# Layer 1's loop with four engine queues tied to program order, and a step that starts with work from the step before

## The chip, the cores and the metric

The program runs on one core of one Trainium2 chip. The metric is the device time of one execution in microseconds; the kernel before takes 18878.0 us (median of three runs, 18847.7 to 18889.9). A core has five instruction queues that matter here: PE (matmul and transpose), DVE (vector), ACT (scalar, activation functions), POOL (GpSimd) and SP, which issues most of the DMA transfers. Each engine runs its own stream of instructions and waits on semaphores where it needs another engine's result.

## The reference, cut to what matters

The input x has the shape (4, 512, 512, 16). Each layer normalises by groups of two channels, applies a convolution and adds its input. Layer 0 is a global convolution in the Fourier domain. The change concerns layer 1 alone, a 3x3 convolution whose output passes through an arc cosine and two tanh factors:

```python
input_norm = jnp.sqrt(lax.conv_general_dilated(x * x, ones_f, strides, 'SAME', ...) + EPS)
kernel_norm = jnp.sqrt(jnp.sum(kernel * kernel, axis=(0, 1, 2), keepdims=True) + EPS)
y = lax.conv_general_dilated(x, kernel / kernel_norm, strides, 'SAME', ...)
y = y / input_norm
y = 1.0 - jnp.arccos(y) * (2.0 / jnp.pi)
y = y * (jnp.tanh(kernel_norm / radius) * jnp.tanh(input_norm / radius))
...
x = x + _L1_conv_ref(_gn(x), ...)
```

The group norm needs mean and variance over a whole image, so the statistics of an image must be complete before its first block enters layer 1. The arc cosine is evaluated as a square root times a polynomial in |y|.

## The kernel before

The program runs the phases of layer 0 (filter, forward, convolution in frequency), then `last_phase`: an inverse transform that writes the layer-0 result by channel to DRAM (L1096 to L1108), and then the loop of layer 1, which starts at about 17116 us of the span. Only this loop is touched.

**Beside the loop: `prepare()` (L994).** A Python generator makes x + layer 0 for every image and its statistics. For one tile of 128 rows by 128 columns it loads x and two halves of the layer-0 result (`p_x`, `p_y`, L1001 and L1005, two buffers each), adds them on POOL (L1026, twice), takes 16 bn_stats on DVE (L1022), and writes the tile to DRAM (`t_d`, L1034). After 16 tiles it aggregates and finishes the image's mean and variance (L1041 to L1068). Image 0 is finished before the loop. The statistics of the other three images run beside it: one `next(beside, None)` (L1331) per step.

**The loop.** The output of an image is cut into groups of 32 columns and four units of 128 rows each: 256 units in 64 groups over four images. Input comes in blocks of eight columns by 16 channels, transposed so that the partitions hold (column, channel). Each unit passes through these functions, and a step u of `step(u)` (L1300) runs each of them for a different unit, so that 14 units are in flight (`lead = 14`):

- `block` (L1134): four transposes on PE (L1138), the normalising activation to `xn` on ACT (L1146), its square `x2` (L1148), a memset on POOL (L1144).
- `squares` (L1159): four matmuls on PE (L1164) that sum squares over channels, a copy on DVE to `e_sum` (L1168), and in two steps of four a small copy on POOL (L1170, L1173).
- `over_w` (L1175) and `norms` (L1181), once per group: two additions on POOL (L1177, L1178), three matmuls on PE (L1185 to L1187), a square root and, for every second group, tanh on ACT (L1192, L1194), a reciprocal on DVE (L1196).
- `border` (L1207), once per group: copies on POOL (L1214), four transposes on PE (L1217), memsets on POOL, and three operations on DVE (L1226).
- `conv` (L1230): 12 matmuls (24 in the profile[...]; L1234) and one for the edges (L1242), into the PSUM tile `pc`, of which there are four.
- `cosine` (L1250): one multiplication on DVE (L1252).
- `root` (L1255): Abs, Relu and Sqrt on ACT (L1258 to L1260). `factors` (L1263): three Squares and a Sign on ACT (L1268, L1270).
- `gate` (L1273) and `signed` (L1278): one multiplication each on POOL (L1275, L1280).
- `chain` (L1282): five dependent operations on DVE (three on L1286, then L1287 and L1289), which read and write the PSUM tile and end with `e_o`.
- `finish` (L1292): an addition on POOL (L1294) and the output DMA on SP (L1296).

**What sets the order.** The program is written for a framework that records instructions and dependences, and whose scheduler then orders every engine's instructions by its own estimate of when each becomes ready, with program order as priority. Python order in `step` therefore does not fix the order on an engine. In the program before, pieces of different steps are mixed: transposes stand between the matmuls of a conv, and the chains of two units alternate on DVE. Buffers are handed out in turn: `pc` has four, `e_y` and `e_sum` four, `e_v` and `e_o` three, `e_q`, `e_gate`, `pt` two, and the sums of squares `p2` one.

Of the kernel before, what the change touches and what calls it, by code (L numbers as in the profile page):

```python
# [199 lines left out]

def bc(ap, axis, shape):
    return ap.unsqueeze(axis).to_broadcast(shape)

# [711 lines left out]
def last_phase(tc, cst, x, y_d, yw_d, t_d, kern, bias, radius, out):  # L917
    nc = tc.nc
    with ExitStack() as ctx:
# [71 lines left out]
        order = [0, 2, 1, 3]  # L991
# [81 lines left out]
        beside = prepare()  # L1073
# [47 lines left out]
        n_groups = 16 * B  # L1121
        n_units = 4 * n_groups
# [3 lines left out]
        def load(g):  # L1126
            t = xp.tile([P, 4, 32, C], F32, name="xt")
            b, wt, w = order[g // 16], g % 16 // 4, g % 4 * 32
            nc.sync.dma_start(
                out=t, in_=t_d[b][wt].rearrange("(h p) w c -> p h w c", p=P)[:, :, w : w + 32, :]  # L1130
            )
            xt[g] = t

        def block(q):  # L1134

            pt = ps_t.tile([P, N], F32, name="pt")
            for h in range(4):
                nc.tensor.transpose(  # L1138
                    pt[:, h * P : (h + 1) * P],
                    xt[q // 4][:, h, q % 4 * 8 : q % 4 * 8 + 8, :].rearrange("p w c -> p (w c)"),  # L1140
                    ident,
                )
            xn = np_.tile([P, N + 2], F32, name="xn")
            nc.gpsimd.memset(xn[:, 0 : N + 2 : N + 1], 0.0)  # L1144
            vec = vecs[order[q // 64]]
            nc.scalar.activation(xn[:, 1 : N + 1], pt, AF.Identity, scale=vec[:, 0:1], bias=vec[:, 1:2])  # L1146
            x2 = ew.tile([P, N], F32, name="x2")
            nc.scalar.activation(x2, xn[:, 1 : N + 1], AF.Square)  # L1148
            xns[q], x2s[q] = xn, x2
# [9 lines left out]
        def squares(q):  # L1159

            g, k = q // 4, q % 4
            p2 = ps_s.tile([P, 4, 8], F32, name="p2", tag="gn_ps")
            for h in range(4):
                nc.tensor.matmul(p2[:, h], x2s[q][:, h * P : (h + 1) * P], cols, start=True, stop=True)  # L1164
            del x2s[q]
            if g not in sums:
                edges(g)
            nc.vector.tensor_copy(sums[g][:, :, 1 + 8 * k : 9 + 8 * k], p2)  # L1168
            if k == 0 and g % 16 > 0:
                nc.gpsimd.tensor_copy(sums[g - 1][:, :, 33:34], sums[g][:, :, 1:2])  # L1170
            if k == 3 and g % 16 < 15:
                edges(g + 1)
                nc.gpsimd.tensor_copy(sums[g + 1][:, :, 0:1], sums[g][:, :, 32:33])  # L1173
# [7 lines left out]
        def norms(g):  # L1181

            s3 = st["s3"]
            pn = ps_n.tile([P, 4, 32], F32, name="pn")
            nc.tensor.matmul(pn, over_h[:, 0], s3, start=True, stop=False)  # L1185
            nc.tensor.matmul(pn[:, 1:4], over_h[:, 1], s3[:, 0:3], start=False, stop=False)
            nc.tensor.matmul(pn[:, 0:3], over_h[:, 2], s3[:, 1:4], start=False, stop=True)  # L1187
            if g % 2 == 0:
                st["inn"] = ew.tile([P, 2, 4, 32], F32, name="l_inn")
                st["th"] = ew.tile([P, 2, 4, 32], F32, name="l_th", bufs=4)  # L1190
            inn, th = st["inn"], st["th"]
            nc.scalar.activation(inn[:, g % 2], pn, AF.Sqrt, bias=eps1)  # L1192
            if g % 2:
                nc.scalar.activation(th, inn, AF.Tanh, scale=rrad)  # L1194
            rin = ew.tile([P, 4, 32], F32, name="l_rin", bufs=4)
            nc.vector.reciprocal(rin, inn[:, g % 2])  # L1196
            rins[g], ths[g] = rin, th[:, g % 2]
# [9 lines left out]
        def border(g):  # L1207

            t = ew.tile([P, 4, 3, 2, C], F32, name="e_bx")
            for side in range(2):  # L1210
                at, w = (g + 2 * side - 1, 31 - 31 * side)
                if at // 16 != g // 16 or at < 0:
                    at, w = g, 0
                nc.gpsimd.tensor_copy(t[:, :, :, side], bc(xt[at][:, :, w, :], 2, [P, 4, 3, C]))  # L1214
            pt = ps_t.tile([P, N], F32, name="pt")
            for h in range(4):
                nc.tensor.transpose(pt[:96, h * P : (h + 1) * P],  # L1217
                                    t[:, h].rearrange("p d s c -> p (d s c)"), ident)
            bx = ew.tile([96, N], F32, name="e_bn")
            nc.gpsimd.memset(bx[0:32, 0:1], 0.0)  # L1220
            nc.gpsimd.memset(bx[64:96, N - 1 : N], 0.0)
            vec = vecs[order[g // 16]]
            for dh in range(3):
                r = slice(32 * dh, 32 * dh + 32)
                lo, hi = max(1 - dh, 0), min(N + 1 - dh, N)
                nc.vector.tensor_scalar(bx[r, lo:hi], pt[r, lo + dh - 1 : hi + dh - 1],  # L1226
                                        vec[r, 0:1], vec[r, 1:2], ALU.mult, ALU.add)
            borders[g] = bx

        def conv(u):  # L1230
            h, ts = u % 4, list(terms(u // 4))
            pc = ps_c.tile(sh, F32, name="pc")
            for n, (q, dh, lo, hi, o) in enumerate(ts):
                nc.tensor.matmul(  # L1234
                    pc[:, lo:hi, :].rearrange("p w j -> p (w j)"),
                    xns[q][:, h * P + dh : h * P + dh + P],
                    bands[dh][:, o : o + hi - lo, :].rearrange("p w j -> p (w j)"),
                    start=(n == 0), stop=False,
                )

            lo, hi = int(u // 4 % 16 == 0), 2 - int(u // 4 % 16 == 15)
            nc.tensor.matmul(  # L1242
                pc[:, 31 * lo : 31 * hi - 30 : 31, :],
                borders[u // 4][:, h * P : (h + 1) * P], eband[:, lo:hi], start=False, stop=True,
            )
            if h == 3:
                del borders[u // 4]
            pcs[u] = pc
# [6 lines left out]
        def root(u):  # L1255

            v = ew.tile(sh, F32, name="e_v", bufs=3)
            nc.scalar.activation(v, st["y", u], AF.Abs)  # L1258
            nc.scalar.activation(v, v, AF.Relu, scale=-1.0, bias=1.0)
            nc.scalar.activation(pcs[u], v, AF.Sqrt, scale=ARC[7] ** 2)  # L1260
            st["v", u] = v
# [16 lines left out]
        def signed(u):  # L1278
            t = st["gate", u]
            nc.gpsimd.tensor_mul(t, t, st.pop(("y", u)))  # L1280

        def chain(u):  # L1282

            r = pcs.pop(u)
            for q, (_, rest) in zip(st.pop(("q", u)), ARC_PAIRS):
                nc.vector.scalar_tensor_tensor(r, q, rest, r, ALU.add, ALU.mult)  # L1286
            nc.vector.scalar_tensor_tensor(r, st.pop(("v", u)), ARC_ROOT - 1.0, r, ALU.add, ALU.mult)  # L1287
            o = ew.tile(sh, F32, name="e_o", bufs=3)
            nc.vector.scalar_tensor_tensor(o, r, -1.0, st.pop(("gate", u)), ALU.add, ALU.mult)  # L1289
            st["o", u] = o  # L1290
# [7 lines left out]
        lead = 14  # L1298

        def step(u):  # L1300
            if u % 4 == 0 and (u + lead) // 4 + 2 < n_groups:
                load((u + lead) // 4 + 2)
            if 0 <= u + lead - 1 < n_units:
                squares(u + lead - 1)

            g, k = divmod(u + lead - 3 - 4, 4)
            if k == 0 and 0 <= g < n_groups:
                norms(g)
            if u + lead < n_units:
                block(u + lead)  # L1310
            if u % 4 == 2 and 0 <= u + 6 < n_units:
                border((u + 6) // 4)
            if 0 <= u + 3 < n_units:
                conv(u + 3)
            if 0 <= u < n_units:
                signed(u)
            if 0 <= u - 1 < n_units:
                finish(u - 1)
            if 0 <= u + 1 < n_units:
                root(u + 1)  # L1320
                gate(u + 1)
                factors(u + 1)
            if 0 <= u < n_units:
                chain(u)
            if 0 <= u + 2 < n_units:
                cosine(u + 2)
            g, k = divmod(u + lead - 2 - 4, 4)
            if k == 0 and 0 <= g < n_groups:
                over_w(g)
            if u >= 0:  # L1330
                next(beside, None)  # L1331
            for q in [q for q in xns if q < u]:
                del xns[q]

# [1 line left out]
            next(beside)  # L1336
        for g in range(3):
            load(g)
        for u in range(-lead, n_units + 1):
            step(u)  # L1340


def body(tc, ins, cst, out):
# [47 lines left out]
```

## Time and profile before

| | |
|---|---|
| median of three runs | 18878.0 us |
| profiled execution | 18884.85 us, its span 18883.1 us |
| PE busy over the span | 17055.0 us (90%) |
| DVE, ACT, POOL busy | 11526.1 (61%), 9724.0 (51%), 11616.7 us (62%) |
| mean granted PE clock | 0.957 |
| layer-1 loop, first transposes to the end | 17116 to 18883 us |

The span is the profiler's own window of the execution; some 2 us of the execution lie around it. Busy shares of the whole span are means over phases with different limits: in the loop of layer 1, from 17154 us on, PE, DVE and ACT are all busy most of the time. Rows of a timeline give the start and the duration in us, the engine, the line, the operation with its output and inputs, and in brackets the idle time before it and what ended that idle time. A list of waits gives the total in us, how often, and the longest.

### The profile page before, as it was taken

Reading aid. Unit: us, or ns where it says so; the run is one execution under the profiler, and the core shown is the slowest. Engines: PE = TensorE matmul, PEld = TensorE weight load, DVE = VectorE, ACT = ScalarE, POOL = GpSimd, SP = SyncE. Lnnn points to the kernel's source line nnn. Section 1 sums busy time; section 2 is a strip of 40 time slices with the busy share of each in tenths; the row PEclk is TensorE's granted clock in tenths of the full one; section 3 lists DMA queues with packets and bytes.
Section 4 is the critical chain, followed back from the end, with each engine's and each line's share of the span. In section 5 each row is a group of like instructions: output and inputs, shape, how many; then the busy total and the mean of one; then the engine's idle time right before and its main releaser. Section 6 shows DMA issues by size and latency. Waiting matters only on the chain. (4 is left out here: it accounts for less than half of the span.)

```text
span 18883.1 us, 533095 instructions
## 1 busy us (share of the span) xinstructions
PE 17055.0 (90%) x224908; PEld 12368.5 (66%) x224908; DVE 11526.1 (61%) x24155; ACT 9724.0 (51%) x17871; POOL 11616.7 (62%) x12701
## 2 busy tenths in 40 slices
PE   7899999999998998988888888888898988988898
PEld 5455555555554457777777777777777776877777
DVE  8877777777773335555555555555555555246887
ACT  4455555555552235555555555555555554005788
POOL 7577777777771126666666666666666666026776
PEclk8899999999999999999999999999999999998999
DMA  3755555455547668888888888888888888696432
GB/s 101 207 153 141 144 150 150 134 152 152 147 140 230 187 199 321 325 319 320 322 323 318 324 318 320 322 323 321 323 322 320 324 324 306 248 326 208 161 127 71
DMA packets 2918838, 4543.16 MB, mean 241 GB/s; under 512 B 117634, under 2 KB 2086492, under 8 KB 2809566
## 3 DMA queue, kind: packets, MB, share of 16 engines
q1 hardware_dynamic: 2686254, 3768.92, 59.1%
q0 software_dynamic: 174896, 605.89, 8.3%
q10 hardware_dynamic: 55296, 134.24, 2.1%
q8 instruction: 1773, 29.05, 0.6%
q14 instruction: 619, 5.07, 0.1%
HBM read 3031.24 MB, written 1477.31 MB: 239 GB/s over the span
## 5 line engine op out<-in xcount | busy, mean ns | idle before, releaser
L783 PE MATMUL pg<-c_dg,g 64*128 64x128 f32 x32832 | 2855.2, 291 | 347.3 <-ACT gh L683 193.2
L799 PE MATMUL pm<-xe,gh 128*32 128x64 f32 x131328 | 2394.6, 222 | 555.4 <-issue 297.3
L799 PEld LDWEIGHTS pm<-xe,gh 128*32 128x32 f32 x131328 | 2011.6, 111 | 1153.2 <-issue 962.1
L783 PEld LDWEIGHTS pg<-c_dg,g 64*128 64x128 f32 x32832 | 2292.4, 190 | 695.3 <-issue 257.2
L372 PE MATMUL pg<-c_dinv,sp 128*128 128x256 f32 x8192 | 2279.4, 426 | 296.0 <-ACT st L377 179.1
L828 DVE TENSOR_TENSOR z<-zq,pz 128x256 f32<-128x256 f32 x2052 | 861.8, 420 | 2665.9 <-ACT zq L827 2591.7
L348 DVE RECIPROCAL dn<-dn 128x256 f32<-128x256 f32 x1024 | 1790.8, 1749 | 774.7 <-POOL dn L341 774.6
L372 PEld LDWEIGHTS pg<-c_dinv,sp 128*128 128x128 f32 x8192 | 1611.1, 207 | 944.3 <-issue 213.0
L681 DVE COPY gh<-pg 128x512 f32<-128x512 f32 x2046 | 1410.0, 689 | 1247.7 <-PE pg L783 1244.0
L417 PE MATMUL pt<-ev_in,c_todd 128*128 128x512 f32 x4096 | 1974.9, 607 | 51.9 <-DMA ev_in<-g_d 27.3
L752 POOL TENSOR_TENSOR xu<-xe,c_late 128x256 f32<-128x256 f32 x2052 | 1393.7, 705 | 893.1 <-ACT xe L683 866.3
L683 ACT COPY yf<-pm 128x512 f32<-128x512 f32 x2046 | 1210.9, 592 | 935.8 <-PE pm L799 921.5
L335 ACT COPY ab<-pab 128x512 f32<-128x512 f32 x2048 | 1103.9, 591 | 1126.3 <-POOL m L355 323.9
L377 ACT COPY st<-pg 128x256 f32<-128x256 f32 x2048 | 1072.6, 622 | 1025.4 <-PE pg L372 629.3
L763 ACT COPY xe<-xl 64x1024 f32<-64x1024 f32 x513 | 538.6, 1050 | 1891.4 <-POOL xl L754 1891.4
L350 POOL TENSOR_TENSOR x<-ab,ab 128x256 f32<-128x256 f32 x1024 | 874.7, 854 | 922.9 <-ACT ab L335 896.4
L683 ACT COPY gh<-pg 128x512 f32<-128x512 f32 x2058 | 1201.1, 584 | 392.3 <-PE pg L783 383.0
L820 PE MATMUL pz<-c_ident,yf 128*128 128x128 f32 x8208 | 1373.7, 290 | 29.8 <-issue 28.0
L417 PEld LDWEIGHTS pt<-ev_in,c_todd 128*128 128x128 f32 x4096 | 807.5, 198 | 680.0 <-issue 518.2
L329 PEld LDWEIGHTS pab<-c_e,u 18*128 18x128 f32 x8192 | 719.0, 187 | 806.1 <-ACT st L377 458.3
L754 POOL TENSOR_TENSOR xl<-xl,xu 128x1024 f32<-128x1024 f32 x513 | 1209.7, 2358 | 40.2
L329 PE MATMUL pab<-c_e,u 18*128 18x256 f32 x8192 | 1186.5, 406 | 5.6 <-ACT ab L335 5.6
(205 smaller groups left out, 33831.8 us busy)
## 6 DMA issues: line engine op xcount, KB each, us to landing
xe<-xf_d SPq DMA_DIRECT2D x1026, 1536.0 KB, 10.7
g<-g_d SPq DMA_DIRECT2D x511, 1024.0 KB, 9.9
g_d<-st SPq DMA_DIRECT2D x64, 4096.0 KB, 34.5
ev_in<-g_d SPq DMA_DIRECT2D x1024, 256.0 KB, 4.8
g_d<-ot SPq DMA_DIRECT2D x1024, 256.0 KB, 2.8
xf_d<-xe POOLq DMA_DIRECT2D x513, 448.0 KB, 8.4
xf_d<-xl POOLq DMA_DIRECT2D x513, 448.0 KB, 5.4
x_d<-xo SPq DMA_DIRECT2D x128, 1024.0 KB, 5.1
```

Source lines behind the costliest of these rows:

```text
L329: nc.tensor.matmul(pp[n][:, k].rearrange("p c n -> p (c n)"), w["us"][n][q, k1 : k1 + P], e2[q, n, w["h"], :], start=True, stop=True,)
L335: nc.scalar.copy(w["ab"][n], pp[n])
L348: nc.vector.reciprocal(w["dn"], w["dn"])
L372: nc.tensor.matmul(pg[:, k].rearrange("p a x -> p (a x)"), w["sp"][:, k, c, :], dinv[:, 2 * kp + k, c, :], start=(c == 0), stop=(c == 1),)
L417: nc.tensor.matmul(pt, todd[:, c, kc, hh * P : hh * P + P], ev[:, kc, c], start=(kc == 0), stop=(kc == 1),)
L681: nc.vector.tensor_copy(dst, src)
L683: nc.scalar.copy(dst, src)
L752: nc.gpsimd.tensor_mul(u[:, :, h, c], xe[:, :, h, 1 - c], bc(late[:, 1 + c], 2, [P, F, 2]))
L754: nc.gpsimd.tensor_add(xl.rearrange("p f h c k -> p (f h c k)"), xl.rearrange("p f h c k -> p (f h c k)"), u.rearrange("p f h c k -> p (f ...
L783: nc.tensor.matmul(pg[c][:, j % 4], g[half, j], dg[half], start=True, stop=True)
L799: nc.tensor.matmul(pm[32 * q : 32 * q + 32, g % 8], gh[:, f].rearrange("p c j -> p (c j)"), xe[:, :, f].rearrange("p t h c k -> p t (h c k ...
L820: nc.tensor.transpose(pz[:, t % 4].rearrange("p v q x -> p (v q x)"), y[:, at].rearrange("p g x -> p (g x)"), ident)
```

## The change

A small class ties the instructions that a block of code records to program order on chosen engines. Each instruction of such an engine gets an ordering edge to the one recorded before it on the same engine; the edge adds no semaphore. The loop runs `step(u)` inside it, with PE, DVE, ACT and POOL chosen. SP is not chosen. The load of a group and `next(beside, None)` move out of `step` and stay untied. Inside `step` the written order, which now is the order on each engine, is changed: `signed(u)`, `chain(u)` and `root(u + 1)`, whose inputs come from the step before, stand first.

```diff
+class InOrder:
+    def __init__(self, tc, *engines):
+        self.tc, self.last, self.depth = tc, {}, 0
+        self.engines = [e.engine for e in engines]
+
+    def __enter__(self):
+        self.begin = len(self.tc.nc.cur_bb.bb.instructions)
+
+    def __exit__(self, *_):
+        dep = mybir.DependencyInfo(mybir.DependencyClass.NoSync, mybir.DependencyReason.DATA)
+        for i in list(self.tc.nc.cur_bb.bb.instructions)[self.begin :]:
+            if i.engine in self.engines:
+                if i.engine in self.last:
+                    self.tc.add_manual_dep(i, self.last[i.engine], dep, reason="in order")
+                self.last[i.engine] = i.name
...
         def step(u):
-            if u % 4 == 0 and (u + lead) // 4 + 2 < n_groups:
-                load((u + lead) // 4 + 2)
+            if 0 <= u < n_units:
+                signed(u)
+                chain(u)
+            if 0 <= u + 1 < n_units:
+                root(u + 1)
             if 0 <= u + lead - 1 < n_units:
                 squares(u + lead - 1)
...
                 conv(u + 3)
-            if 0 <= u < n_units:
-                signed(u)
             if 0 <= u - 1 < n_units:
                 finish(u - 1)
             if 0 <= u + 1 < n_units:
-                root(u + 1)
                 gate(u + 1)
                 factors(u + 1)
-            if 0 <= u < n_units:
-                chain(u)
             if 0 <= u + 2 < n_units:
                 cosine(u + 2)
...
                 over_w(g)
-            if u >= 0:
-                next(beside, None)
...
+        pinned = InOrder(tc, nc.tensor, nc.vector, nc.scalar, nc.gpsimd)
         for u in range(-lead, n_units + 1):
-            step(u)
+            if u % 4 == 0 and (u + lead) // 4 + 2 < n_groups:
+                load((u + lead) // 4 + 2)
+            with pinned:
+                step(u)
+            if u >= 0:
+                next(beside, None)
```

So the order on each engine within a step becomes, in the program as built: PE squares, norms, block, border, conv; DVE chain, the copy of the squares, reciprocal, border, cosine; ACT root, the norms' square root and tanh, block, factors; POOL signed, the small copies, memset, border copies, finish, gate, over_w.

## The prediction

> **What bounds the kernel now.** I first read the busy time of each engine by stage. Cutting the layer-1 loop where its character changes gives the four rows below (columns: stretch and length in us, then busy us of PE, PEld, DVE, ACT and POOL with counts, then clock, DMA share, GB/s). The chain that ended last lies inside this loop too, but it only names the last 480 us, so I worked from waits and timelines.
>
> ```profile
> 17154.00:17525.00 371.00, 315.38 (x2114) 279.44 (x2114) 286.04 (x583) 290.63 (x498) 268.27 (x331) 0.91 0.52 165
> 17525.00:18180.00 655.00, 572.82 (x3831) 504.77 (x3830) 544.00 (x1110) 533.75 (x918) 496.85 (x606) 0.93 0.52 168
> 18180.00:18788.00 608.00, 552.02 (x3793) 489.92 (x3792) 466.50 (x789) 519.17 (x891) 379.05 (x561) 0.96 0.22 77
> 18788.00:18883.00 95.00, 69.39 (x470) 60.92 (x467) 76.49 (x123) 81.04 (x139) 66.95 (x66) 0.94 0.14 53
> ```
>
> See: PE is nearest to full (91% in the third row), ACT next (85%). Counting the starts of L1252 gives the unit's pace: unit 0 at 17154, 52 at about 17525, 240 at 18788. That is 371/52 = 7.13 us a unit, and 1263 us for units 52 to 240: 7.0 each while the statistics of the next images run beside (until 18180), 6.45 after (51.6 us per 8 units, exactly periodic). From unit 240 no new block is fetched and a unit takes 4.06 us.
>
> Next the waits, in the two stretches 17200 to 18000 and 18200 to 18800 (us in total, times, longest):
>
> ```profile
> PE pn L1185 <- POOL e_sum L1178: 83.7, 28, 9.4
> PE pc L1234 <- DVE e_o L1289: 24.7, 34, 3.0
> ```
> ```profile
> PE pn L1185 <- POOL e_sum L1178: 36.1, 23, 2.6
> PE pc L1234 <- DVE e_o L1289: 14.2, 21, 1.5
> ```
>
> So PE stands still before the norms because POOL is late, and before conv because the chain (L1286 to L1289) is late: (83.7 + 24.7)/114 = 0.95 us a unit early, (36.1 + 14.2)/93 = 0.54 late. That is what there is to win on PE: 6.45 - 0.54 = 5.9.
>
> Two details of the timeline price the rest. ACT issues independent neighbours 0.52 us apart, but Relu after its own Abs 0.64:
>
> ```profile
> 18847.44 0.61 ACT L1258 ACTIVATE e_v<-e_y 128x512 f32<-128x512 f32 x1
> 18848.08 0.63 ACT L1259 ACTIVATE e_v<-e_v 128x512 f32<-128x512 f32 x1
> 18848.62 0.61 ACT L1270 ACTIVATE e_y<-e_y 128x512 f32<-128x512 f32 x1
> ```
>
> And after a long PE wait the conv is slow, 6.29 instead of some 3.9 us:
>
> ```profile
> 17506.76 0.80 PE L1185 MATMUL pn<-e_sum,c_over_h 128*128 128x128 f32 x2 [3.59 <-POOL e_sum L1178]
> 17507.35 6.29 PE L1234 MATMUL pc<-l_band,xn 128*128 128x512 f32 x24
> ```
>
> [...] conv stands behind the waiting L1185. [...] 3.59 us is followed by a 6.29 us conv, a 1.52 us gap by 3.98.
>
> **The change, part by part.** In the order of instructions of the two built programs all stages before the loop are the same, so only 17116 to 18883 can move. I call a step by u mod 4: border stands in 2, norms in 1, over_w in 0.
>
> *a. Beside work is crowded into the front.* The statistics (L1022, L1026, their DMAs) are not pinned. In the order of before, 496 bn_stats and 62 adds follow the first cosine, spread to unit 148. In the changed order 483 and 58 stand before unit 57: 8.9 bn_stats and 1.1 adds a step. DVE a step: six 128x512 operations 0.60 apart (3.6), copy 0.15, border 2.44/4, reciprocal 0.86/4, bn_stats 8.9 x 0.285 (ten take 2.82) = 7.1. POOL: L1280 + L1294 + L1275 = 1.28 + 1.27 + 1.06, small ones 0.6, adds 1.1 x 2.87 = 7.4. Both exceed today's 7.13. POOL's queue is now in order: adds (two together are 5.7 us) stand before L1280 or before L1178, and behind those wait L1289 on DVE, then the copy L1168, then the squares on PE (one p2 buffer), or the norms. Walking four steps with five adds I get 34 us, POOL busy 92%; with the mean 4.3 adds, 29.3/0.92 = 31.9, 8.0 a step. PE then idles over 3 us in one place, one slow conv (+2.4) per four steps: 8.6. The p_x loads keep two buffers and a tile every 15 us: write 5.0 + load 5.3 us fit, without much to spare. 52 x 8.6 = 447 against 371: **+76**. Bounds: 7.6 (queues always full) to 9.8 (each tile also waits for its DMA).
>
> *b. The late loop.* ACT a step in its new order: Abs 0.64, Relu 0.65, Sqrt 0.53, xn 0.81 (its square now follows directly), square 0.52, three q 1.84, Sign 0.52 = 5.51; plus L1192 0.25/4, and tanh with two table loads 3.24/8: **5.98**. PE: conv 4.03, squares 0.9, transposes 0.45, norms 0.8/4, border 0.52/4 = 5.7. DVE, chain now dependent (0.78 apart): 5.3. POOL 4.2. If nothing waited, ACT would set 6.0. But one step in four has a new wait: POOL's border copies (L1214) come behind the copy L1173, which waits for DVE's L1168, which stands behind the whole chain. Take xn of step 1 as 0: Sign ends 3.79, L1280 ends 5.17, chain (first q at 2.05; five operations) reaches L1289 at 5.31, L1168 5.92, L1173 6.2, L1214 twice to 7.15. PE's border transposes start at 7.3; PE was ready at 5.2. Then 0.52 + 4.03 + 0.9 + 0.45, and xn of step 3 can start at 13.35; ACT alone would be there at 11.04, DVE (border 2.44, cosine, then root) lets it at 12.97. From step 3 to the next step 1: ACT 11.5, or 13.1 with tanh. Eight steps: 2 x 13.35 + 11.5 + 13.1 = 51.3, **6.41** a step: the wait on over_w goes (POOL is done 1.9 us ahead of the norms) and the border wait takes its place. 188 x 6.41 = 1205 against 1263: **-58**, nearly all of it the beside work that left units 52 to 148. The ordering edges themselves carry no semaphore, so no instruction gains a wait from them beyond its place in the queue. The finish, its output DMA and the next loads hide: SP waited 644 us for L1294 already, and the xt loads keep their place in SP's order.
>
> *c. The ramp.* Before, PE mixes conv pieces into the first 38 us (17116 to 17154). Now each of eleven steps is a closed round: transposes 1.0, xn 0.81, square 0.62, squares 1.7 (cold, as at 17123), hops 0.3: 4.4 x 11 = 48, norms and border 5, the DMA wait 6 as before, first conv 4: 63 against about 41 with the same wait inside: **+22** (15 to 40).
>
> *d. The tail.* 14 steps at ACT 4.2 to DVE 4.33 instead of 4.06, and about 3 us at the end because cosine stands behind a chain: **+7**.
>
> Sum: 76 - 58 + 22 + 7 = +47. The profiled execution took 18884.9 (span 18883.1); the median is 18878.0, and I put the sum on the median: **18925**.
>
> **Rivals.**
> *Late loop at the ACT limit (faster).* If the border copies are served early, PE does not stall and a step costs ACT's 6.0: 188 x 6.0 = 1128, -135; with the front at 8.0 (+45) and c, d: 18878 - 135 + 45 + 29 = 18817. For: PE and ACT totals allow it; the wait at L1185 is real. Against: the written order above. It decides below 6.16 us a step: there the late loop pays back c, d and the front's 76 (1263 - 105 = 1158 over 188).
> *The crowded front costs more (slower).* At 10 us a step, because in-order adds also wait for DMA (L1026 waited 22.5 us for p_x at a third of the rate): 520 - 371 = +149, total 18878 + 149 - 58 + 29 = 18998.
> *Nothing to see.* The scheduler's order was already near this one and gains cancel: 18878. Against: the two orders differ in every step.
>
> **How the numbers follow.** A measurement of this kernel can tell about 0.2%, 38 us. Forecast 0.45 (0.33 of it beyond +0.2%, 0.12 within), crowded front 0.25 (slower), ACT limit 0.20 (0.16 faster, 0.04 within), cancelling 0.10 (0.07 within, 0.02 slower, 0.01 faster): faster 0.17, same 0.23, slower 0.60. Ends: front 7.6 to 9.8 (+24 to +139), late 6.0 to 6.7 (-135 to -3), ramp and tail +20 to +45: 18787 to 19059 if all fall together; leaving a tenth on each side, 18840 to 19030. The forecast's own range is 18890 to 18965.
>
> **What would show it.** Right: bn_stats gone by about unit 55; units there about 8.6 us apart, later 6.4; no wait of L1185's counterpart on POOL late, but PE border transposes waiting about 2 us on POOL e_bx once in four steps; the first cosine 20 us later. Wrong: a late step under 6.1 or above 6.7; PE waiting elsewhere late (squares on the DVE copy); a front faster than 7.6, which would mean POOL and DVE do not bind each other.

## The result, and the profile after

The changed kernel takes 19031.1 us (median of three runs, 19027.0 to 19055.8), against 18878.0 before: ratio 1.009, 95% interval 1.0076 to 1.0104. It is slower by about 153 us; 47 us were forecast.

The stages below answer to the four rows of the kernel before; the columns are the same (stretch, length, busy us of PE, PEld, DVE, ACT and POOL, clock, DMA share, GB/s). The cuts lie again near the cosine of unit 0 (17166), of unit 52 (17646) and of unit 240 (18937).

```profile
17166.00:17646.00 480.00, 352.30 (x2107) 307.98 (x2106) 380.31 (x907) 311.26 (x501) 368.14 (x368) 0.81 0.75 239
17646.00:18937.00 1291.00, 1127.47 (x7624) 1002.87 (x7623) 953.88 (x1567) 1119.70 (x1813) 762.71 (x1131) 0.92 0.22 77
18937.00:19029.00 92.00, 66.70 (x448) 59.44 (x447) 74.42 (x113) 75.16 (x124) 63.39 (x67) 0.89 0.14 52
```

The reader is to see that in the middle row, where after its first 20 us hardly anything runs beside the loop any more, no engine is full: PE 87%, ACT 87%, DVE 74%, POOL 59%. So the engines wait for one another. The spans differ by 19029.1 - 18883.1 = 146 us, and the stages give it back, predicted beside measured:

| stage | predicted, us | measured, us |
|---|---|---|
| ramp, to the first cosine | +22 | 17166.4 - 17154.0 = +12 |
| units 0 to 52 | +76 (8.6 a unit) | 480 - 371 = +109 (9.2) |
| units 52 to 240 | -58 (6.41 a step) | 1291 - 1263 = +28 (6.87) |
| units 240 to the end | +7 | 92 - 95 = -3 |

In the periodic part the cosines come 54.7 us per eight units, 6.83 each. The largest miss, 86 of 99 us, is in units 52 to 240, the late step. (Against the kernel before, most of the added time, 109 of 146 us, is in units 0 to 52, partly because work beside has moved there.) The waits of the changed kernel between 18300 and 18700, some 58 units (us in total, times, longest):

```profile
PE pt L1236 <- POOL e_bn L1239: 43.8, 15, 3.9
ACT xn L1165 <- POOL xn L1163: 36.2, 21, 2.6
POOL e_sum L1189 <- DVE e_sum L1187: 44.3, 14, 3.5
PE pn L1204 <- POOL e_sum L1197: 0.7, 2, 0.3
```

Lines are 19 higher than before: L1236 are the border transposes, L1165 is the activation that makes `xn`, L1163 the memset of its two edge columns, L1189 the `e_sum` copy (L1170 before), L1187 DVE's copy of the squares, L1204 the norms. The wait of the norms has gone, as said. The border transposes wait once in four steps, as said, but 43.8/15 = 2.9 us and not about 2. And ACT waits for a memset of 0.1 us, which no step of the prediction had. How this comes about, in one step of the timeline of the changed kernel (in brackets the idle time before, and what ended it). First the way through DVE and POOL:

```profile
18505.59 0.69 DVE L1308 SCALAR_TENSOR_TENSOR e_o<-pc,e_gate 128x512 f32<-128x512 f32 x1
18506.20 0.18 DVE L1187 COPY e_sum<-p 128x32 f32<-128x32 f32 x1
18506.44 0.19 POOL L1189 COPY e_sum<-e_sum 128x4 f32<-128x4 f32 x1 [3.08 <-DVE e_sum L1187]
18506.57 0.11 POOL L1163 MEMSET xn<- 128x2 f32 x1
18506.71 0.78 ACT L1165 ACTIVATE xn<-pt,l_vec 128x512 f32<-128x512 f32 x1 [2.18 <-POOL xn L1163]
```

Read it from the top: the chain's last operation, the copy of the squares behind it on DVE, the `e_sum` copy on POOL that needs it, the memset behind that on POOL, and then `xn`, which needs the memset. POOL had been idle for 3.08 us and ACT for 2.18. From `xn` the same step goes on to the three q (L1287), and these feed the next chain: a loop through ACT, DVE and POOL.

Then the way through PE to the same `xn`. The rows begin two steps earlier, with the `xn` that the prediction calls step 1; they show the border transposes, the border operations on DVE with the chain behind them, the conv, and the transposes (the second L1157) that the `xn` at 18506.71 reads:

```profile
18491.36 0.76 ACT L1165 ACTIVATE xn<-pt,l_vec 128x512 f32<-128x512 f32 x1
18493.75 0.64 PE L1157 MATMUL pt<-c_ident,xt 128*128 128x128 f32 x4
18498.29 1.09 PE L1236 MATMUL pt<-c_ident,e_bx 128*96 128x128 f32 x4 [3.91 <-POOL e_bn L1239]
18499.18 5.86 PE L1253 MATMUL pc<-l_band,xn 128*128 128x512 f32 x24
18499.42 2.44 DVE L1245 TENSOR_SCALAR e_bn<-pt,l_vec 32x511 f32<-32x511 f32 x3 [2.04 <-PE pt L1236]
18502.48 2.29 DVE L1305 SCALAR_TENSOR_TENSOR pc<-e_q,pc 128x512 f32<-128x512 f32 x3
18505.91 0.63 PE L1157 MATMUL pt<-c_ident,xt 128*128 128x128 f32 x4
```

PE waits 3.91 us for the border copies, the conv behind them takes 5.86 us instead of 3.88, and the transposes end at 18506.54. The memset ends at 18506.68. So the list names the memset, which came last, but without it `xn` could have started only some 0.1 us earlier: two late ways meet here (the ends of matmuls are modelled in the profile, so tenths of a microsecond are rough). Over the 21 waits of `xn` in the list, the transposes of its block were done for only 15.8 of the 36.2 us; for the rest they were late as well.

My theory after this: the tiny POOL operations behind the `e_sum` copy hold ACT and PE, and cost some 0.8 us a step. The rivals: the strict order of dependent operations on ACT and DVE sets the pace by itself; the tie does so whatever the order of the step; the border wait is the missing time alone.

### The profile page after: what moved, and what is told of

Read it like the earlier page. It is cut to its first block, busy times and chain, and to the rows that moved or that the text cites. A ratio compares the mean times of both kernels' runs of the same rounds, so it can differ in the third digit from the quotient of the medians.

```text
span 19029.1 us, 533073 instructions
## 1 busy us (share of the span) xinstructions
PE 17104.2 (90%) x224908; PEld 12412.9 (65%) x224908; DVE 11562.6 (61%) x24155; ACT 9806.2 (52%) x17871; POOL 11591.7 (61%) x12701
```

## The experiments

Late steps are the distance of the cosine's starts between units 144 and 240 (168 and 240 where the statistics last longer), divided by the units. The ramp is the time before the first cosine, the front units 0 to 52; a yield is one call of `next(beside)`. Absolute times come from several chips, so each run is held against the kernel before on its own chip.

| run | edit | late step, us | ratio to before | 95% interval |
|---|---|---|---|---|
| before | | 6.49 | 1 | |
| changed kernel | | 6.83 | 1.0090 | 1.0076 to 1.0104 |
| e1_memset | memset a step ahead | 6.58 | 1.0057 | 1.0042 to 1.0072 |
| e2_border | border copies a step ahead | 6.38 | 1.0046 | 1.0031 to 1.0060 |
| e3_both | both | 5.99 | 0.9997 | 0.9988 to 1.0006 |
| e13_joins | `e_sum` copies after the border | 6.41 | 1.0042 | 1.0027 to 1.0056 |
| e7_order_only | no tie | 6.23 | 0.9989 | 0.9982 to 0.9996 |
| e6_tie_old | tie, old order | 6.69 | 1.0065 | 1.0050 to 1.0080 |
| e10_old_both | e6_tie_old and both moves | 6.34 | 1.0016 | 1.0008 to 1.0024 |
| e8_lead_free | ramp not tied | 6.83 | 1.0079 | 1.0062 to 1.0096 |
| e11_spread | statistics spread | 6.81 | 1.0073 | 1.0056 to 1.0089 |
| e5_all | e3_both, one yield a step | 5.99 | 0.9971 | 0.9959 to 0.9982 |
| e9_spread_all | e3_both, spread | 5.99 | 0.9959 | 0.9945 to 0.9974 |
| e12_spread_lead | e9_spread_all, ramp not tied | 5.99 | 0.9959 | 0.9944 to 0.9974 |

### One tiny operation at a time

e1_memset records the memset for the next block at the end of the step before:

```diff
-            xn = np_.tile([P, N + 2], F32, name="xn")
-            nc.gpsimd.memset(xn[:, 0 : N + 2 : N + 1], 0.0)
+            xn = xns[q]
...
+        def blank(q):
+            xn = np_.tile([P, N + 2], F32, name="xn")
+            nc.gpsimd.memset(xn[:, 0 : N + 2 : N + 1], 0.0)
+            xns[q] = xn
...
+            if u + lead + 1 < n_units:
+                blank(u + lead + 1)
```

> Only the memset of xn's edge columns moves: for the block of the next step it is recorded at the end of the step before, so the activation xn no longer stands behind signed and the e_sum copy on POOL. Theory (memset on POOL closes a loop through the step): the waits of ACT xn on POOL go, the late step falls from 6.84 to about 6.4 us (the border waits of about 3 us per four steps stay), the front gains a little as well; about 18950 us (18920 to 18990). Rival (strict order of the dependent operations on ACT and DVE alone sets the pace): the waits move to another line, the step stays at 6.8, 19030 us.

Measured: 1.0057, late step 6.58. The wait of `xn` on POOL is gone; the border wait is untouched (41.7 us in 15 times). About half of the gain that I gave this part, because ACT now waits for the other way (between 18300 and 18700):

```profile
ACT xn L1164 <- PE pt L1157: 16.6, 15, 1.9
```

The 0.25 us a step agree with the 15.8 us for which the memset alone had held `xn` (15.8/58 = 0.27).

e2_border does the same for POOL's share of the border:

```diff
+        def sides(g):
+            t = ew.tile([P, 4, 3, 2, C], F32, name="e_bx")
...
+            st["b", g] = t, bx
...
+            if u % 4 == 1 and 0 <= u + 7 < n_units:
+                sides((u + 7) // 4)
```

> Only POOL's border copies and memsets move: recorded at the end of the step before the border's step. Theory: the waits of PE's border transposes (3.05 us each in four steps) and the slow conv after them go, but xn still waits on the memset, so the gain is part of what both give: late step about 6.6 us, 18985 us (18940 to 19030). Rival (the border wait alone is the missing time): late step 6.0, 18880 us.

Measured: 1.0046, late step 6.38, more than the theory gave it and less than the rival. The order of the two sizes was wrong: the border is the larger part. The waits of the profile say why the two aren't independent. With the border served early, `xn` waits as often as before but shorter (before the move 36.2 us):

```profile
ACT xn L1165 <- POOL xn L1163: 19.9, 21, 1.2
```

The late border makes DVE's border operations late, these the chain of the next step, and that chain the `e_sum` copy and the memset, as the rows of the changed kernel show (L1236, L1245, L1305, L1308, L1187, L1189, L1163).

e3_both is the two edits together.

> Both moves together. Theory: nothing on ACT's or PE's path stands behind the e_sum copy any more; the late step comes to the limit of ACT, about 6.05 us against 6.84, 188 steps x 0.79 = 150 us, total about 18880 us (18840 to 18910). Rival (strict order of the dependent operations): 19000 us or more, late step over 6.7.

Measured: 0.9997, late step 5.99: both moves give the whole loss back, 0.84 us a step, where singly they gave 0.25 and 0.45. In the list of waits of this run between 18300 and 18700 ACT no longer appears. The busy time of the same stretch, the changed kernel and then e3_both:

```profile
18300.00:18700.00 400.00, 349.78 (x2374) 310.82 (x2373) 294.26 (x480) 347.35 (x565) 235.81 (x353) 0.93 0.22 76
```

```profile
18300.00:18700.00 400.00, 376.42 (x2706) 339.26 (x2706) 329.42 (x534) 393.42 (x644) 271.02 (x403) 1.00 0.25 87
```

The fourth pair is ACT: 347 of 400 us become 393, 98%. ACT is the bound, at 5.99 us a step; the prediction had worked out 5.98 for it, from operations in the trace of before. The strict order of dependent operations is inside these 5.99, so as a cause of the loss it falls. The clock column rises too, from 0.93 to 1.00: a part of the gain is faster convs (last section), and no run separates the waits from the clock.

### Which operation holds them

Memset and border copies stand behind two waiting operations on POOL: `signed`, which waits for ACT's Sign, and the `e_sum` copy. e13_joins takes only the second away: the copies are recorded after the border.

```diff
-            if k == 0 and g % 16 > 0:
-                nc.gpsimd.tensor_copy(sums[g - 1][:, :, 33:34], sums[g][:, :, 1:2])
             if k == 3 and g % 16 < 15:
                 edges(g + 1)
-                nc.gpsimd.tensor_copy(sums[g + 1][:, :, 0:1], sums[g][:, :, 32:33])
...
                 border((u + 6) // 4)
+            if 0 <= u + lead - 1 < n_units:
+                joins(u + lead - 1)
```

> The changed kernel with one thing moved: the two small e_sum copies on POOL are recorded after the border instead of with the squares, so the memset of xn and the border copies still stand behind signed, but no longer behind a copy that waits for DVE's copy of the squares behind the chain. Theory (that e_sum copy is what holds the memset and the border copies): late step 6.0 to 6.2 us, ratio near 0.9997 as e3_both (to 1.002). Rival (signed, which waits for ACT's Sign, is what holds them): late step 6.8, ratio 1.009. Between the two: each holds some of the steps.

Measured: 1.0042, late step 6.41, between the two: each holds a part. Waits of PE and ACT in this run between 18300 and 18700:

```profile
PE pt L1240 <- POOL e_bn L1243: 30.0, 16, 2.8
ACT xn L1165 <- PE pt L1157: 18.4, 16, 2.2
```

ACT doesn't wait for the memset any more, and the border transposes (L1240 here) wait 30.0/16 = 1.9 us, behind `signed`. The length is the one that the prediction gave, 6.41 us, but not its step: there the border copies waited 1.0 us for the `e_sum` copy (5.17 to 6.2), which here stands behind them, and the conv ran at full speed, while in this run 9 of the 55 convs that the timeline from 18300 to 18690 gives as one whole row take 5.25 to 6.24 us. That the two numbers agree is luck. Of the 0.84 us, 0.42 belong to the place behind the `e_sum` copy; the other 0.42 go only when memset and border copies leave their place behind `signed` too.

### The tie and the order

e7_order_only takes the tie away and leaves the order of `step`:

```diff
-            with pinned:
-                step(u)
+            step(u)
```

> The new order of step without the tie: the scheduler places every instruction by its own estimate. Theory (the loop needs the strict queue): the waits of xn and of the border on POOL are small, the total is near the kernel before, 18880 us (18840 to 18930). Rival (the order of the step alone is what costs, tied or not): 19030 us.

Measured: 0.9989, late step 6.23, without a wait of `xn` on POOL. The rival falls: the order costs nothing by itself, since the scheduler doesn't hold to it.

e6_tie_old ties the engines, with the calls of `step` in the order of before:

```diff
         def step(u):
-            if 0 <= u < n_units:
-                signed(u)
-                chain(u)
-            if 0 <= u + 1 < n_units:
-                root(u + 1)
...
                 conv(u + 3)
+            if 0 <= u < n_units:
+                signed(u)
...
             if 0 <= u + 1 < n_units:
+                root(u + 1)
                 gate(u + 1)
                 factors(u + 1)
+            if 0 <= u < n_units:
+                chain(u)
```

> The tie with the order of the step before: signed, root and the chain stand where they stood, so the copy of the squares comes ahead of the chain on DVE and the memset and the border copies ahead of signed on POOL. Theory (the order of the changed step, under the tie, is what puts xn and the border behind the chain): no such waits, late step 6.0 to 6.4 us, total about 18890 us (18840 to 18950). Rival (tied queues cost by themselves, whatever the order): late step 6.8 or more, 19030 us or more.

Measured: 1.0065, late step 6.69: my expectation missed. I had thought that with the copy of the squares ahead of the chain nothing would be late. But in the queue that copy stands behind the previous step's chain and cosine, and the memset again behind the `e_sum` copy. Timeline of this run:

```profile
18500.97 0.68 DVE L1271 TENSOR_TENSOR e_y<-pc,l_rin 128x512 f32<-128x512 f32 x1
18501.56 0.18 DVE L1187 COPY e_sum<-p 128x32 f32<-128x32 f32 x1
18501.81 0.19 POOL L1189 COPY e_sum<-e_sum 128x4 f32<-128x4 f32 x1 [4.01 <-DVE e_sum L1187]
18501.93 0.11 POOL L1163 MEMSET xn<- 128x2 f32 x1
18502.07 0.78 ACT L1165 ACTIVATE xn<-pt,l_vec 128x512 f32<-128x512 f32 x1 [2.93 <-POOL xn L1163]
```

So the number is nearer to the rival "the tie costs whatever the order", though below its 6.8. To part the tie from the tiny operations, e10_old_both adds the two moves to it.

> The tie with the step order of before, and the memset and the border copies recorded a step ahead as in e3_both. Theory (the small POOL operations behind the e_sum copy are the cost in either order): late step 6.0 to 6.2 us against 6.67 in e6_tie_old, ratio about 0.9997 as e3_both. Rival (the old order under the tie has a slower step of its own, the changed order is needed too): late step 6.4 us or more, ratio 1.003 or more.

Measured: 1.0016, late step 6.34: between the two. The moves gain 0.35 us here as well, about half of what e6_tie_old has over the 5.99 of e3_both, which is tied too. So the tie as such isn't what e6_tie_old paid for. The other 0.35 us remain, and the waits show one that the old order keeps: the reciprocal waits on DVE for ACT's square root, which the changed order doesn't do in e3_both (us in total, times, longest, over about 63 units). That this wait is the 0.35 us was not tried:

```profile
DVE l_rin L1219 <- ACT l_inn L1215: 33.2, 16, 3.8
```

With the tie and the two moves, then, the changed order is the better one.

### The front and the ramp

e8_lead_free leaves the steps before -2 untied.

```diff
-            with pinned:
-                step(u)
+            if u < -2:
+                step(u)
+            else:
+                with pinned:
+                    step(u)
```

> The changed kernel with the steps of the ramp (those before step -2) left untied. Theory (the tied order serialises the first blocks): the first cosine comes at about 38 us after the first transposes as before instead of 58, total lower by 12 to 20 us, about 19013 us. Rival (the ramp is set by its operations, not by the tie): 19030 us.

Measured: 1.0079, not resolved from 1.0090. From the first transposes to the first cosine it took 17189.0 - 17150.3 = 39 us, as in the kernel before, instead of 17166.4 - 17099.7 = 67 (the expectation had left out the first block and its wait); but the total didn't get these 28 us. The front gives most of them back: from the first transposes to the cosine of unit 52 it is 537 us, against 546 in the changed kernel. e12_spread_lead below asks again with less around it.

e11_spread changes only when the statistics run: 45 yields ahead of the loop, then one in two steps of three, inside the tie.

```diff
+        for _ in range(45):
+            next(beside)
...
             with pinned:
                 step(u)
-            if u >= 0:
-                next(beside, None)
+                if u >= 0 and u % 3:
+                    next(beside, None)
```

> The changed kernel with only the pacing of e9_spread_all: 45 yields ahead of the loop, then one at the end of two steps of three inside the tied block; memset and border stay behind the e_sum copy. Theory (crowding the statistics into 56 steps costs by itself): about 7.2 us x 156 + 6.84 x 84 = 1698 us for units 0 to 240 against 1771, total about 18960 us, ratio 1.005. Rival (they cost the same wherever they stand): ratio 1.009.

Measured: 1.0073, an interval that overlaps the one of the changed kernel. In the profile, units 0 to 168 take 18441.6 - 17181.9 = 1260 us against 18446.2 - 17166.4 = 1280: a gain of 20 us, where I had given 73. Spread or crowded, some 500 bn_stats and their additions cost about the same on top of 6.83 us a step: 1260 - 168 x 6.83 = 113 us spread, and 128 crowded (units 0 to 56: 511 - 56 x 6.83).

e5_all moves the yields of e3_both into the tie, one a step.

```diff
             with pinned:
                 step(u)
-            if u >= 0:
-                next(beside, None)
+                if u >= 0:
+                    next(beside, None)
```

> e3_both, and the call that advances the statistics moves inside the tied block, so one of its yields stands at the end of every step, over some 152 steps, instead of where the scheduler puts it (96 steps in e3_both, 56 in the changed kernel). Theory (statistics that are crowded into few steps cost more than spread ones, since DVE then has more than ACT): DVE about 5.3 + 0.95 = 6.3 us a step while they last, so 6.5 x 152 + 6.0 x 88 = 1516 us for units 0 to 240 against 1595 in e3_both, total about 18765 us (18720 to 18850). Rival (in a tied queue an addition of 2.87 us and eight bn_stats of 2.3 us stand ahead of signed and the chain, and hold the step up): 7.5 us a step while they last, total 18915 us.

Measured: 0.9971. The units up to 144 take 1048 us, 7.28 each, nearer the rival. But I had also forgotten that the scheduler does part of the statistics ahead of the loop: from 17100 on there are 744 bn_stats in e5_all and 496 in e3_both, so both expectations stood on the wrong amount. e9_spread_all therefore takes the spread of e11_spread on top of e3_both.

> e5_all, but 45 yields of the statistics are drawn ahead of the loop and one at the end of two steps of three after that, so that the loop has as many bn_stats as the changed kernel, spread over about 156 steps. Theory (work beside costs by its amount per step): DVE 5.3 + 0.6 us a step, the step about 6.6 us while they last instead of 7.0 in e5_all, about 60 us less than e5_all, which was 0.9971 of the kernel before: ratio about 0.994. Rival (draws ahead of the loop delay its start as much): the first transposes come later, ratio 0.997.

Measured: 0.9959 (0.994 expected). Up to unit 144 a step takes (18167.4 - 17200.1)/144 = 6.72 us. Per bn_stats in that time, that is 0.73 x 144/480 = 0.22 us over the 5.99 of a step without them; in e5_all it is 1.29 x 144/728 = 0.26, so most of what e5_all pays more is the amount. From the cosine of unit 0 to that of unit 255 it takes 18833.0 - 17200.1 = 1633 us, against 18865.9 - 17154.0 = 1712 before and 18825.8 - 17156.3 = 1670 in e3_both: 79 us less than before, which is 0.42% of 18878 and fits the ratio. It isn't work moved ahead of the loop: after the first cosine there are 512 bn_stats, and 496 before the change. e3_both is 42 us shorter in the same measure, but its timed ratio shows no gain. The late step is 5.99 in four kernels on three chips; if the rest of the loop is as steady, the 42 us were lost ahead of the first cosine, but no trace of the kernel before on that chip shows it.

e12_spread_lead is e9_spread_all with the steps before -2 outside the tie, as in e8_lead_free.

> e9_spread_all with the steps of the ramp (before step -2) untied. Theory (the tie serialises the first blocks, and with paced statistics the gain isn't given back): the first cosine comes some 10 to 20 us earlier after the first transposes, total 10 to 20 us less than e9_spread_all. Rival (the ramp is set by its operations): no difference.

Measured: 0.9959 again. The first cosine comes 39 us after the first transposes instead of 63, but at the same time: 17198.3 against 17200.1. Only the transposes began earlier under the tie. The rival holds: what comes before sets the first cosine, not the closed rounds of the ramp.

So e9_spread_all beats both kernels: tie and new order kept, memset and border copies a step ahead, statistics at a steady rate. Whether it needs the tie is open: e7_order_only, without it, measures 0.9989, and the steady statistics were not tried there.

## Why the prediction was wrong

- **Direction: right. The step that failed: in step b, the way from `xn` of step 1 to `xn` of step 3.** Step b said that the wait on the norms would go and a border wait take its place. Both show. It gave 13.35 us to the two steps around the border; on average they take 15.1. The two steps after them came out as reckoned: 11.3 us and, with tanh (its two table loads, on ACT, take 1.28 us each), 13.2, against 11.5 and 13.1. So a late step is 6.83 us and not 6.41: +28 us where -58 was predicted, 86 of the 99 us between forecast and profile.
- **What stood in its place.** In the rows above, counted from `xn` at 18491.36, POOL is nearly where the walk had it: the border transposes start at 6.93, said was 7.3. Two ways from there to `xn` of step 3 were too short. On PE, the walk let PE wait 2.1 us and then gave the border transposes and the conv 0.52 + 4.03 us. PE was ready at 3.03 and not at 5.2, waited 3.91, and the two took 1.09 + 5.86, though step a had priced a slow conv behind a long PE wait at +2.4. On POOL, the walk stopped at the border copies. The memset L1163 is queued behind both `e_sum` copies, in two steps of four, and `xn` waits for it. I had counted the memset among POOL's 4.2 us of work and not as something that ACT waits for. The walk assumed that nothing passes a waiting instruction in a tied queue. The rows bear that out: on POOL the memset of 0.11 us doesn't pass the copy that waits 3.08 us. Both ways reach `xn` of step 3 at over 15 us instead of 13.35: the transposes end at 15.18, the memset at 15.32. So one move alone gave only a part back.
- **The rival of the ACT limit: its condition was right.** "If the border copies are served early" a step should cost ACT's 6.0. With the memset served early too, it does: 5.99 in e3_both. With the border alone, 6.38. The rival was put at 0.20 for a kernel in which its condition didn't hold.
- **Front.** 9.2 us a unit against 8.6 (bounds 7.6 to 9.8), 33 us more than predicted. The same two waits stand at the head of the list between 17240 and 17600, longer than late; that they make the difference was not tried by itself (e3_both takes 399 us for the front instead of 479, but has fewer of the statistics in it: 286 bn_stats up to unit 56 instead of 483):

```profile
ACT xn L1165 <- POOL xn L1163: 103.7, 30, 9.3
PE pt L1236 <- POOL e_bn L1239: 50.9, 9, 7.3
```

The heading "crowded" was misleading: e11_spread shows that crowding makes about 20 us of difference. Most of the +76 in step a is work beside that was moved from later units, as the -58 of step b already said.
- **Ramp.** +12 in the profile against +22; with the statistics spread, e12_spread_lead shows no cost of the tied ramp in the total. The count of 4.4 us a round came near the ramp's length (67 us measured, 63 said), but its beginning had moved forward too, from 17116.2 to 17099.7. The squares of 1.7 us that c calls cold stand in the kernel before at a granted clock of 0.50 (17123 to 17130).
- **Tail.** -3 against +7: 14 steps were no slower than before.
- **Range.** The late bound of 6.7 us took the known waits with a little more; the memset and the slow conv in the same two steps lay beyond it. The sign named for it, a late step above 6.7, is what came.

## What to carry to other kernels

In the tied queues here, an operation behind one that waits inherited the wait, however small (a memset of 0.11 us behind a copy that waited 3.08 us): list them all, with who reads each of them on any engine, and not only the one that looks heavy. A memset or copy that depends on nothing recent can be recorded a step ahead; here this turned a loss of 0.9% into none, and with the work beside at a steady rate into a gain of 0.4%. Two late operations in one loop are not two prices: removed singly they gave 0.25 and 0.45 us a step, together 0.84. A list of waits names the operation that came last; look when the others that the same instruction needs were done, since that bounds what its removal can gain by itself.

## What the hardware showed that was not expected

**Slow convs need no long wait.** The prediction took slow convs as the result of long PE waits, from a wait of 3.59 us before a conv of 6.29. In the changed kernel it looks so too: a wait of 3.91 us, then a conv of 5.86, at a granted clock of 0.66 (a conv of 3.88, from 18487.92, has 1.00). But the kernel before has no PE wait over 1.72 us between 18300 and 18690 and e2_border none over 1.5, and both have slow convs: of the convs that the timeline between 18300 and 18690 gives as one whole row, 10 of 54 in e2_border take over 4.6 us, against 9 of 52 in the changed kernel, 8 of 54 before, and none of 57 in e3_both. One of e2_border's:

```profile
18501.88 1.06 PE L1183 MATMUL p<-c_cols,x 128*128 128x8 f32 x8 [1.02 <-ACT x L1167]
18502.79 0.90 PE L1157 MATMUL pt<-c_ident,xt 128*128 128x128 f32 x4
18503.48 5.34 PE L1258 MATMUL pc<-l_band,xn 128*128 128x512 f32 x24
```

A wait of 1.02 us stands before it. The granted clock between 18300 and 18700 is 0.93 in the changed kernel, 0.94 in e2_border, and 1.00 in e3_both, where PE waits little and evenly. Two neighbouring windows of 3.41 us in e2_border (columns as in the rows of the stages):

```profile
18499.61:18503.02 3.41, 2.39 (x21) 2.28 (x20) 1.59 (x4) 2.60 (x5) 2.46 (x4) 1.00 0.18 70
18503.02:18506.43 3.41, 3.41 (x12) 2.38 (x11) 3.04 (x7) 3.35 (x7) 2.11 (x3) 0.50 0.02 7
```

PE was busy for 70% of the first, at a clock of 1.00; the second, in which the conv starts, had 0.50. The traces of the kernel before and of the changed one, each laid out in 146 windows of 3.4133 us from 18252.93 and 18250.63, give a count: 11 and 23 of them show a clock of 0.50, the others 1.00. Of the windows at 1.00 with another behind them, 35 had PE busy for under 69%, and 25 of these were followed by one at 0.50; of nine from 69 to 75%, one was; of 212 above that, none. So in these traces a fall of the clock follows a window in which PE was busy for under 75%, and in e2_border's rows no more stands before it than a wait of 1.02 us and short operations; why ten of the 35 were not followed by one, these runs don't say. In the changed kernel the long border waits and the slow convs stand together: of the 15 convs behind border transposes between 18300 and 18690, 12 are slow (convs whose rows are cut counted too), and no others. The nine that stand as whole rows are worth 14.7 us over 3.9 us each, 0.25 us a unit at least, so part of the gain of e3_both is the clock.

**A memset of 0.1 us on a path of 6 us.** L1163 touches two columns of 128 partitions. Where it stood was worth 0.25 us a step with the border late, and 0.39 with the border early (6.38 to 5.99, the clock's share of it included).
